# Attention with softmax differences: the sums of every second unit taken early by ScalarE, and both softmaxes joined ahead of one value product

## The chip, the cores and the metric

The kernel runs on one core of a Trainium2 chip, in fp32 throughout (some operands are rounded to fp32r and carried as a high and a low part). The metric is the device time of one execution in microseconds, the median of several runs. The engines are called as in the profile: PE (TensorE matmuls), PEld (its weight loads), DVE (VectorE), ACT (ScalarE), POOL (GpSimd) and SP (SyncE, which issues most DMAs).

## What is computed

The input x is 8 x 1024 x 512. One transformer block is applied: attention on the normalised x, added to x, then a feed-forward part on the normalised result, added again. The attention has 16 heads of width 32; each head's queries and keys are split into two halves of 16, which give two softmaxes, and their difference multiplies the values:

```python
a1 = jax.nn.softmax(jnp.einsum('bhsd,bhtd->bhst', q1, k1) * scale, axis=-1)
a2 = jax.nn.softmax(jnp.einsum('bhsd,bhtd->bhst', q2, k2) * scale, axis=-1)
lam = jnp.exp(jnp.dot(lambda_q1, lambda_k1)) - jnp.exp(jnp.dot(lambda_q2, lambda_k2)) + LAMBDA_INIT
a = a1 - lam * a2
out = jnp.einsum('bhst,bhtd->bhsd', a, v)
rms = jnp.sqrt(jnp.mean(out * out, axis=-1, keepdims=True) + EPS)
out_n = out / rms * norm_w[None, :, None, :] * (1.0 - LAMBDA_INIT)
```

The feed-forward part has ternary weights, a squared ReLU and a low-rank term. The change doesn't touch it.

## The kernel before

**Start (to 138 us).** The first batch entry is normalised, turned and projected; the feed-forward weights are made ternary and written to DRAM beside it. Under the last 16 projections the score maxima of the first two units are taken.

**The attention loop (138 to 4262 us, line 594).** A unit `u` is half the queries (512) of one head of one batch entry; there are NU = 256. Even and odd units of a head share its keys (`tk`, line 177). A unit has eight key chunks `kc` of 128 keys, and one pass of the loop, called a step here, treats two of them; so a unit has the steps kc=0, 2, 4 and 6. In each step stand, in the order in which every engine's queue gets them (the order of the code; the engines PE, ACT, DVE and POOL are not reordered, line 592):

1. `evict` (line 305) of the unit that ended in the step before: ACT copies `acc` to `avs`, scaled by 1 or -lambda.
2. `max_scores` (line 197) for the unit two ahead (AHEAD = 16 chunks): PE makes scores `mx` of 128 queries x 512 keys for both softmaxes (line 207), and DVE takes their negative maxima `nm` (line 218). The three PSUM banks of `ps_mx` go round. The second product of the first pair is put between those of `exp_scores`.
3. `exp_scores` (line 253), twice: PE adds minus the maximum (`nms`, a product with `one2`) and the transposed scores of 128 keys x 512 queries into a bank `one` (line 267; four banks, which all other work shares), and ACT writes the exponentials into `e` (line 273). No sum is taken there.
4. `add_up` (line 279): POOL adds `e` over the chunks into `es` (lines 283 and 285), three operations of 128x2048 per unit, in the steps kc=2, 4 and 6.
5. The second `max_scores` of the step.
6. In the steps kc=0 (and some kc=4): pieces of the next batch entry's preparation. Long ones are `project` (line 151, product in line 157) and `value_tile` (142, product in 145); short ones normalise and turn a tile. Further `max_turn` (230), which turns the maxima, splits them and sends them through DRAM to `nms`; `heads_out` (318) of the unit three before; and `sums` (310) of the unit two before.
7. `values` (line 296): PE multiplies the exponentials of the step before with the values. Four products of 32 output rows stand side by side in `acc` (`quarters`, line 287): two query halves for each of two softmaxes, 256 columns each.

`sums` multiplies `es` with ones, likewise in quarters. `heads_out` turns the products and the sums (four transposes), and DVE divides each softmax's part by its sum and adds the two (lines 334 to 347). Every fourth unit is followed by the RMS norm of four units: squares on ACT (358), sums on DVE, `rms_apply` on POOL (lines 368, 369 and 371, in the step kc=2 of an even unit), and `output_rows` (375) in the step kc=4 of an odd unit.

**The feed-forward part (from 4262 us).** PE runs products in lines 744 to 763, with ReLU on ACT (line 752), the square on POOL (753) and a split in two parts on DVE.

Other lines that are used below: 88 (an exponential of 128x2 on ACT), 870 (absolute values of the weights on ACT, with an accumulated sum), 877 (a fused operation of two tensors on DVE), 961 (a copy of 128x128 on ACT).

Of the kernel before, what the change touches and what calls it, by code (L numbers as in the profile page):

```python
# [24 lines left out]
def block_phases(  # L25
# [45 lines left out]
    one2 = wpool.tile([P, P], F32R, name="one2")  # L71
    nms = [wpool.tile([P, HS], F32R, name=f"nms{i}") for i in range(3)]
    for t in (one2, *nms):
        nc.gpsimd.memset(t.bitcast(F32), 0.0)
# [4 lines left out]
    def constants(stage):  # L79
        lam_in = stage.tile([P, 4, HD], F32, name="lam_in")  # L80
        for i, src in enumerate((lq1, lq2, lk1, lk2)):
            nc.sync.dma_start(lam_in[:, i, :], src.partition_broadcast(P))
        lam_pr = stage.tile([P, 2, HD], F32, name="lam_pr")
        nc.vector.tensor_mul(lam_pr, lam_in[:, 0:2, :], lam_in[:, 2:4, :])
        lam_s = stage.tile([P, 2], F32, name="lam_s")
        nc.vector.tensor_reduce(lam_s, lam_pr, AX.X, ALU.add)
        lam_e = stage.tile([P, 2], F32, name="lam_e")
        nc.scalar.activation(lam_e, lam_s, AF.Exp)

        nc.vector.tensor_sub(one_nlam, lam_e[:, 1:2], lam_e[:, 0:1])  # L90
        nc.vector.tensor_scalar_add(one_nlam, one_nlam, -LAMBDA_INIT)
        nc.vector.memset(one_nlam[0:64, :], 1.0)

        nw_in = stage.tile([P, NHP], F32, name="nw_in")
        for i in range(4):
            nc.sync.dma_start(
                nw_in[HD * i : HD * i + HD, :],
                norm_w.rearrange("(a h) d -> h d a", h=2)[i // 2],
            )
        nc.vector.tensor_scalar_mul(nw, nw_in, 1.0 - LAMBDA_INIT)  # L100
# [93 lines left out]

    nm_of, nm2_of = {}, {}

    def max_scores(u, i, apart=False):

        c, kh = divmod(i, 2)
        if i == 0:  # L200
            nm_of[u] = p_s.tile([P, 2, 2, 4], F32, tag="nm", name="nm", bufs=2)
        mx = [ps_mx.tile([P, 512], F32, tag="mx", name="mx") for _ in range(2)]
# [12 lines left out]

        def post():
            for sm in range(2):
                nc.vector.tensor_reduce(  # L218
                    nm_of[u][:, kh, sm, c : c + 1], mx[sm], AX.X, ALU.max, negate=True
                )  # L220
            if i == 7:
                nm = nm_of.pop(u)
                nm2_of[u] = p_s.tile([P, 8], F32, tag="nm2", name="nm2", bufs=2)
                nc.vector.tensor_reduce(
                    nm2_of[u], nm.rearrange("p k s c -> p (s c) k"), AX.X, ALU.min
                )

        return (lambda: product(1), post) if apart else post

    def max_turn(u):  # L230
        tr = one_bank()
        nc.tensor.transpose(tr[0:8, 0:P], nm2_of.pop(u), ident)

# [41 lines left out]
    def light(u):  # L275

        return u >= NU - 2 * H and (u % 2 == 1 or u >= NU - 3)

    def add_up(u, kc):
        e = e_of[u, kc // 2]  # L280
        if kc == 2:
            es_of[u] = p_es.tile([P, 2, 2, HS], F32, tag="es", name="es")
            nc.gpsimd.tensor_add(es_of[u], e_of[u, 0], e)  # L283
        elif kc == 4 or kc == 6 and not light(u):
            nc.gpsimd.tensor_add(es_of[u], es_of[u], e)  # L285
# [10 lines left out]
    def values(u, kc):  # L296
        b, h = divmod(u // 2, H)
        if kc == 0:
            acc_of[u] = ps_acc.tile([P, 512], F32, tag="acc", name="acc")[:, 0 : HS // 2]
        quarters(  # L300
            acc_of[u], v_of[b][:, kc, h * HD : (h + 1) * HD], e_of[u, kc // 2][:, kc % 2],
            kc == 0, kc == NS - 1,
        )

    def evict(u):
        avs_of[u] = p_s.tile([P, 2, HS // 2], F32, tag="avs", name="avs", bufs=4)

        nc.scalar.activation(avs_of[u][:, 0, :], acc_of.pop(u), AF.Copy, scale=one_nlam)

# [8 lines left out]
    def heads_out(u):  # L318

        avs = avs_of.pop(u)  # L320
        to = one_bank()
        for i in range(2):
            for c in range(2):
# [5 lines left out]
        def post():  # L329
# [6 lines left out]
            for sm, o in enumerate((parts[:, 0, 0], o2)):  # L336
# [4 lines left out]
                )  # L341
            n = u // 4
            if u % 4 == 0:
                og_of[n] = p_o.tile([P, 4, P], F32, tag="og", name="og")
            col = (u % 4) * HD
            og = og_of[n][:, :, col : col + HD]
            nc.vector.tensor_add(  # L347
# [75 lines left out]
    def first_steps():  # L423
# [6 lines left out]
        return steps  # L430

    AHEAD = 16
    def whole(step):
        post = step()
        if post:
            post()
# [3 lines left out]
    with tc.tile_pool(name="a_stage", bufs=1) as stage, tc.manual_schedule(engines=engines):  # L440
# [6 lines left out]
        for blk in range(KC):  # L447
            for which in range(2):
                cols = slice(which * E + blk * P, which * E + blk * P + P)
                nc.sync.dma_start(wqk[:, :, cols], wsrc[:, :, cols])  # L450
        pair_of = {}

# [43 lines left out]
        for i, step in enumerate(steps):  # L496
# [13 lines left out]
            if i == heads - 3:  # L510
                load_keys(0)
                load_queries(0)
            if i >= heads:
                um, im = divmod(i - heads, NS)
                if im == 0:
                    if um > 0:
                        load_keys(um // 2 + 1)
                        posts.append(max_turn(um - 1))
                    load_queries(um + 1)
                posts.append(max_scores(um, im))  # L520
            for post in posts:
                post()
        assert not others and not turns
    p_o = ctx.enter_context(tc.tile_pool(name="a_o", bufs=2))
# [63 lines left out]
    for v in range(NU):  # L588
        adds.setdefault((v + 1, 2) if light(v) else (v + 2, 0), []).append(v)
        outs.setdefault((v + 2, 0) if light(v) else (v + 3, 0), []).append(v)  # L590
    done = None
    ctx.enter_context(tc.manual_schedule(engines=engines))
    with tc.tile_pool(name="a_e", bufs=5) as p_e, tc.tile_pool(name="a_es", bufs=2) as p_es:
        for s in range(0, NS * NU + 2, 2):
            u, kc = divmod(s, NS)
            um, im = divmod(s + AHEAD, NS)
            if done is not None:
# [4 lines left out]
            if u == NU - 1 and kc == 0:  # L602
# [4 lines left out]
                )  # L607
            if um < NU:
                if im == 0 and um + 1 < NU:
                    if um % 2 == 1:  # L610
                        load_keys(um // 2 + 1)
                    load_queries(um + 1)
                between, first = max_scores(um, im, apart=True)
            else:
                between = first = None
            if u < NU:
# [7 lines left out]
                add_up(u, kc)  # L624
            reduce = max_scores(um, im + 1) if um < NU else None
            posts = []
# [5 lines left out]
            if prepare_step and long:  # L632
                posts.append(prepare_step())
            if kc == 0 and um <= NU:
                posts.append(max_turn(um - 1))
            for v in outs.pop((u, kc), []):
# [13 lines left out]
            if reduce:  # L650
                reduce()
            if 2 <= s < NS * NU + 2:
                uv, kv = divmod(s - 2, NS)
# [7 lines left out]
        evict(done)  # L661
        whole(lambda: sums(NU - 1))
    assert not later and list(adds.values()) == list(outs.values()) == [[NU - 1]]

# [401 lines left out]
def block_kernel(  # L1066
    ctx: ExitStack, tc: tile.TileContext, x, w_qkv, wo, lq1, lq2, lk1, lk2, norm_w,
    fast_b, w_fc, w_proj, u, v, gate, out,
):
    nc = tc.nc  # L1070
    B, S, E = x.shape
    cpool = ctx.enter_context(tc.tile_pool(name="consts", bufs=1))
# [41 lines left out]
```

## Time and profile before

| | |
|---|---|
| median of three runs | 5338.41 us (5337.95 to 5341.58) |
| span of the profiled execution | 5338.5 us |
| attention loop, first exponential group to the last | 138 to 4262 us, 4124 us |
| feed-forward part | 4262 to 5338 us |
| busy in the loop: PE, DVE, ACT, POOL | 4091, 3155, 2541, 3744 us |
| mean granted clock of TensorE | 0.999 |
| HBM | 60 GB/s over the span |

How to read it: the span runs from the first to the last instruction, and of the profiled execution nothing but this span is given. Busy time of PE is that of pipelined matmuls, so a full PE row means that its queue doesn't stand still, not that the array is at its peak. In a group of instructions stand the line, engine, operation, output <- inputs, partitions x elements, and the count; then the total busy time, the mean of one in ns, and how long the engine stood idle ahead of them, with what ended it. In a stretch by time, a merged row "x4" is four neighbours in a row, from the start of the first to the end of the last.

### The profile page before, as it was taken

How to read it: one execution, taken by the hardware profiler on the slowest of the kernel's cores; microseconds unless marked ns; L12 is line 12 of the kernel's file. 1: busy time of each engine (PE TensorE's matmuls, PEld its weight loads, DVE VectorE, ACT ScalarE, POOL GpSimd, SP SyncE). 2: the span in 40 equal slices, each digit the busy share in tenths (PEclk: the TensorE clock that was granted, in tenths of full speed). 3: DMA queues.
4: the chain of work that ended last, by engine and by line, in shares of the span. 5: the costliest groups of instructions: out<-in, count | busy, mean ns of one | idle time of the engine just before them, and what ended most of it. 6: DMA issues, size and time to landing. Idle time of an engine off the chain costs nothing.

```text
span 5338.5 us, 105587 instructions
## 1 busy us (share of the span) xinstructions
PE 5280.1 (99%) x41522; PEld 3243.9 (61%) x41522; DVE 3787.7 (71%) x7599; ACT 2832.5 (53%) x5502; POOL 4121.0 (77%) x1495
## 2 busy tenths in 40 slices
PE   8999999999999999999999999999999999999999
PEld 4555555555555555555555555555555578888887
DVE  6877787777778777877777777777888645555554
ACT  4665566566656665666566656655666522222221
POOL 0898899889988998899899989998888733333333
PEclk9999999999999999999999999999999999999999
DMA  8112211211121112111211121112211101111111
GB/s 275 47 55 74 71 50 55 75 66 55 54 77 65 52 57 77 64 55 56 75 65 50 60 81 57 56 61 78 100 48 44 50 31 32 32 32 32 32 32 32
DMA packets 185246, 328.48 MB, mean 62 GB/s; under 512 B 33312, under 2 KB 55840, under 8 KB 184112
## 3 DMA queue, kind: packets, MB, share of 16 engines
q1 hardware_dynamic: 183824, 319.12, 18.3%
q8 instruction: 329, 5.39, 0.4%
q0 software_dynamic: 544, 2.10, 0.1%
q14 instruction: 165, 1.35, 0.1%
q10 hardware_dynamic: 384, 0.52, 0.0%
HBM read 209.16 MB, written 112.46 MB: 60 GB/s over the span
## 4 chain that ended last, share of the span: by engine, by line
PE 84%; POOL 11%; DVE 3%; issue 1%; ACT 1%; DMA 0%; SPq 0%; POOLq 0%; DVEq 0%; ACTq 0%
PE acc L290 15%; PE one L267 14%; PE mx L207 13%; PE y L763 9%; PE pf L744 8%; PE one L157 8%; POOL es L285 6%; PE one L290 4%; PE one L145 4%; PE one L383 3%; POOL es L283 3%; PE one L324 2%; DVE nm L218 1%; PE pf L748 1%; POOL ss L369 1%
## 5 line engine op out<-in xcount | busy, mean ns | idle before, releaser
L218 DVE TENSOR_REDUCE nm<-mx 128x1 f32<-128x512 f32 x4096 | 2550.3, 683 | 256.6 <-PE mx L207 251.5
L273 ACT ACTIVATE e<-one 128x512 f32<-128x512 f32 x4096 | 2116.5, 603 | 803.2 <-PE one L267 751.1
L285 POOL TENSOR_TENSOR es<-es,e 128x2048 f32<-128x2048 f32 x495 | 2261.3, 4568 | 63.2 <-ACT e L273 31.1
L207 PE MATMUL mx<-tk,tq 64*128 64x512 f32 x4096 | 1453.1, 444 | 6.2 <-DVE nm L218 5.6
L283 POOL TENSOR_TENSOR es<-e 128x2048 f32<-128x2048 f32 x256 | 1169.6, 4569 | 278.3 <-ACT e L273 278.2
L267 PE MATMUL one<-nms,one 64*128 64x512 f32 x4096 | 1175.8, 420 | 5.1 <-ACT e L273 2.7
L290 PE MATMUL acc<-e,v 128*32 128x256 f32 x16384 | 1092.7, 384 | 0.0
L207 PEld LDWEIGHTS mx<-tk,tq 64*128 64x128 f32 x4096 | 750.9, 184 | 549.0 <-DVE nm L218 312.3
L267 PE MATMUL one<-tq,tk 64*128 64x512 f32 x4096 | 1063.6, 392 | 0.0
L753 POOL TENSOR_TENSOR r<-r 128x512 f32<-128x512 f32 x256 | 268.4, 1050 | 639.2 <-ACT r L752 618.8
L290 PEld LDWEIGHTS acc<-e,v 128*32 128x32 f32 x16384 | 450.0, 109 | 433.7 <-issue 179.0
L267 PEld LDWEIGHTS one<-tq,tk 64*128 64x128 f32 x4096 | 580.2, 185 | 82.6
L752 ACT ACTIVATE r<-pf,s_fc 128x512 f32<-128x512 f32 x256 | 176.1, 688 | 794.6 <-PE pf L748 544.2
L267 PEld LDWEIGHTS one<-nms,one 64*128 64x128 f32 x4096 | 515.2, 184 | 80.5 <-DVE og L347 15.5
L763 PE MATMUL y<-wpr,r 128*128 128x512 f32 x2048 | 523.3, 397 | 3.7 <-DVE r L757 1.7
L756 DVE CAST r<-r 128x512 fp32r<-128x512 f32 x256 | 180.4, 705 | 425.9 <-POOL r L753 425.9
L157 PE MATMUL one<-hT,wqk 128*128 128x512 f32 x1024 | 475.4, 607 | 1.5 <-ACT hT L138 1.5
L763 PEld LDWEIGHTS y<-wpr,r 128*128 128x128 f32 x2048 | 375.0, 188 | 98.6 <-DVE o L773 20.1
L744 PE MATMUL pf<-hTh,wfc 128*128 128x512 f32 x1024 | 398.8, 389 | 0.0
L744 PE MATMUL pf<-hTl,wfc 128*128 128x512 f32 x1024 | 398.6, 389 | 0.0
L165 DVE SCALAR_TENSOR_TENSOR pc<-one,pc 128x512 fp32r<-128x512 f32 x128 | 88.5, 692 | 350.9 <-ACT pc L164 350.9
L157 PEld LDWEIGHTS one<-hT,wqk 128*128 128x128 f32 x1024 | 185.0, 190 | 217.3 <-issue 187.9
(137 smaller groups left out, 4284.1 us busy)
## 6 DMA issues: line engine op xcount, KB each, us to landing
qk<-pc SPq DMA_DIRECT2D x128, 512.0 KB
tq<-qk SPq DMA_DIRECT2D x512, 128.0 KB
tk<-qk SPq DMA_DIRECT2D x256, 256.0 KB
xs<-in_L_attn_x SPq DMA_DIRECT2D x64, 256.0 KB
xr<-in_L_attn_x SPq DMA_DIRECT2D x256, 64.0 KB
x_dram<-y SPq DMA_DIRECT2D x64, 256.0 KB
out<-o SPq DMA_DIRECT2D x248, 64.0 KB
nms<-md SPq DMA_DIRECT2D x512, 4.0 KB
```

Source lines behind the costliest of these rows:

```text
L145: nc.tensor.matmul(pv, hT_of[b][:, kc, c * P : (c + 1) * P], wv[:, kc, :], start=(kc == 0), stop=(kc == KC - 1),)
L157: nc.tensor.matmul(ps, wqk[:, kc, c0 : c0 + P], hT_of[b][:, kc, tok], start=(kc == 0), stop=(kc == KC - 1),)
L207: nc.tensor.matmul(mx[sm], tq[rows, c * P : (c + 1) * P], tk[rows, kh * 512 : kh * 512 + 512], start=True, stop=True,)
L218: nc.vector.tensor_reduce(nm_of[u][:, kh, sm, c : c + 1], mx[sm], AX.X, ALU.max, negate=True)
L267: nc.tensor.matmul(st[sm], w[rows, cols], m[rows, :], start=(w is one2), stop=(w is not one2))
L273: nc.scalar.activation(e[:, kc % 2, sm, :], st[sm], AF.Exp)
L283: nc.gpsimd.tensor_add(es_of[u], e_of[u, 0], e)
L285: nc.gpsimd.tensor_add(es_of[u], es_of[u], e)
L290: nc.tensor.matmul(out[32 * g : 32 * g + 32, :], w, e[:, g // 2, (g % 2) * (HS // 2) : (g % 2 + 1) * (HS // 2)], start=start, stop=stop,)
L744: nc.tensor.matmul(pf, w[:, kc, :], hT, start=(kc == 0 and i == 0), stop=False)
L753: nc.gpsimd.tensor_mul(r, r, r)
L763: nc.tensor.matmul(ys[i], r2[:, i * P : (i + 1) * P], prep.wpr[j // (NJ // 2)][:, j % (NJ // 2), :], start=(j == 0 and k == 0), stop=(j == ...
```

## The change

Every odd unit (`normal(u)`) is treated in another way; even units stay as they were.

- **Sums taken early.** After DVE has taken the negative maximum of a block of `mx`, ACT takes the exponential of the same block in place, with that maximum as bias, and its accumulator gives the block's sum (`ss1`).
- **Sums joined to the maxima.** `join_sums` scales the two sums of a row (512 keys each) to the common maximum, adds them, takes the logarithm and subtracts it from the negative maximum. What goes through `max_turn` into `nms` is then minus the log-sum, and the exponentials of `exp_scores` are the finished softmax. `sums`, `add_up`'s adds and the division fall away.
- **The softmaxes joined.** `join_softmaxes` forms e1 - lambda e2 (`nlam` is -lambda): for the chunks of kc=0 and 6 POOL does it in two operations, queued by `add_up`; for kc=2 and 4 DVE does it in one, late in the same step. `values` then has one product: four of 32 rows and 128 columns instead of 256. `evict` is a plain copy of 128x128, and `heads_out` one transpose and one copy, two units later.
- **The order of the maxima.** Each step of the loop now has one block pair of an even unit (three units ahead) and one of an odd unit (two to three ahead), instead of two of one unit. Keys and queries are loaded four units ahead of the step, one unit earlier than before. 21 block pairs are done before the loop instead of 16.
- **Light units.** Instead of the last units of the last batch entry that skipped POOL's third add, only unit NU - 2 does.
- **One table.** ACT's function table is loaded at the start by an explicit instruction, with a set that has the exponential and the logarithm.

```diff
+    nlam = p_wo.tile([P, 1], F32, name="nlam")
...
+        nc.vector.tensor_copy(nlam, one_nlam)
...
+    def normal(u):
+        return u % 2 == 1
...
         def post():
+            nm = nm_of[u]
             for sm in range(2):
                 nc.vector.tensor_reduce(
-                    nm_of[u][:, kh, sm, c : c + 1], mx[sm], AX.X, ALU.max, negate=True
+                    nm[:, kh, sm, c : c + 1], mx[sm], AX.X, ALU.max, negate=True
                 )
+            if normal(u):
+                for sm in range(2):
+                    nc.scalar.activation(
+                        mx[sm], mx[sm], AF.Exp, bias=nm[:, kh, sm, c : c + 1],
+                        accum_out=ss1_of[u][:, kh, sm, c : c + 1],
+                    )
...
+    def join_sums(u, part):
+        nm = nm_of[u].rearrange("p k s c -> p k (s c)")
+        ss = ss1_of[u].rearrange("p k s c -> p k (s c)")
+        nm2 = nm2_of[u]
+        if part == 0:
+            dm = dm_of[u] = p_s.tile([P, 2, 8], F32, tag="dm", name="dm", bufs=2)
+            nc.vector.tensor_sub(
+                dm, nm2.rearrange("p (o x) -> p o x", o=1).to_broadcast([P, 2, 8]), nm
+            )
+            nc.scalar.activation(dm, dm, AF.Exp)
+        elif part == 1:
+            nc.vector.tensor_mul(ss, ss, dm_of.pop(u))
+            nc.vector.tensor_add(ss[:, 0], ss[:, 0], ss[:, 1])
+            nc.scalar.activation(ss[:, 1], ss[:, 0], AF.Ln)
+        else:
+            nc.vector.tensor_sub(nm2, nm2, ss1_of.pop(u).rearrange("p k s c -> p k (s c)")[:, 1])
...
     def light(u):
-        return u >= NU - 2 * H and (u % 2 == 1 or u >= NU - 3)
+        return u == NU - 2
+
+    def join_softmaxes(e, eng):
+        e1, e2 = e[:, :, 0], e[:, :, 1]
+        if eng is nc.vector:
+            eng.scalar_tensor_tensor(e1, e2, nlam, e1, ALU.mult, ALU.add)
+        else:
+            eng.tensor_scalar(e2, e2, nlam, None, ALU.mult)
+            eng.tensor_add(e1, e1, e2)
 
     def add_up(u, kc):
         e = e_of[u, kc // 2]
+        if normal(u):
+            if kc in (0, 6):
+                join_softmaxes(e, nc.gpsimd)
+            return
...
     def values(u, kc):
...
+        if normal(u):
+            for g in range(4):
+                nc.tensor.matmul(
+                    acc_of[u][32 * g : 32 * g + 32, 0:P],
+                    v_of[b][:, kc, h * HD : (h + 1) * HD],
+                    e_of[u, kc // 2][:, kc % 2, 0, g * P : (g + 1) * P],
+                    start=(kc == 0), stop=(kc == NS - 1),
+                )
+            return
...
     def evict(u):
+        acc = acc_of.pop(u)
+        if normal(u):
+            avs_of[u] = p_s.tile([P, P], F32, tag="avn", name="avn", bufs=2)
+            nc.scalar.copy(avs_of[u], acc[:, 0:P])
+            return
...
     def heads_out(u):
...
+        if normal(u):
+            nc.tensor.transpose(to[:, 0:P], avs, ident)
+            return lambda: nc.vector.tensor_copy(
+                og, to[:, 0:P].rearrange("p (g d) -> p g d", d=HD)
+            )
...
+    maxima = sorted(
+        (8 * (u // 2) * 2 + 2 * i - (17 if u % 2 else 24), u, i)
+        for u in range(NU) for i in range(NS)
+    )
+    early = [(u, i) for k, u, i in maxima if k < 0]
+    maxima = {k: (u, i) for k, u, i in maxima if k >= 0}
...
+            if kc == 0 and u + 4 < NU:
+                if u % 2 == 0:
+                    load_keys(u // 2 + 2)
+                load_queries(u + 4)
+            between = first = reduce = None
+            if s in maxima:
+                between, first = max_scores(*maxima[s], apart=True)
...
+            if kc == 0 and u % 2 == 0 and u + 1 < NU:
+                join_sums(u + 1, 2)
+            if s + 1 in maxima:
+                reduce = max_scores(*maxima[s + 1])
...
             if reduce:
                 reduce()
+                if kc == 4 and u % 2 == 1:
+                    join_sums(u + 2, 0)
+            if kc == 6 and u % 2 == 1 and u + 2 < NU:
+                join_sums(u + 2, 1)
+            if u < NU and normal(u) and kc in (2, 4):
+                join_softmaxes(e_of[u, kc // 2], nc.vector)
...
+    nc.scalar.add_instruction(
+        mybir.InstLoadActFuncSet(
+            name=nc.get_next_instruction_name(), engine=ET.Activation, act_func_set_id=6
+        )
+    )
```

## The prediction, made before the changed kernel was run

> **What bounds the kernel now.** I read the shares by engine first, then the busy times of the two stages, then the costliest groups, then single steps of the loop in order of time. A step is one pass of the loop in line 594; four make a unit, two units a pair (even, odd).
>
> Page, shares and groups (busy us, mean ns of one, idle time before):
>
> ```profile
> PE 5280.1 (99%) x41522; PEld 3243.9 (61%) x41522; DVE 3787.7 (71%) x7599; ACT 2832.5 (53%) x5502; POOL 4121.0 (77%) x1495
> ...
> L218 DVE TENSOR_REDUCE nm<-mx 128x1 f32<-128x512 f32 x4096 | 2550.3, 683 | 256.6 <-PE mx L207 251.5
> L273 ACT ACTIVATE e<-one 128x512 f32<-128x512 f32 x4096 | 2116.5, 603 | 803.2 <-PE one L267 751.1
> L285 POOL TENSOR_TENSOR es<-es,e 128x2048 f32<-128x2048 f32 x495 | 2261.3, 4568 | 63.2 <-ACT e L273 31.1
> ...
> L752 ACT ACTIVATE r<-pf,s_fc 128x512 f32<-128x512 f32 x256 | 176.1, 688 | 794.6 <-PE pf L748 544.2
> ```
>
> Busy time by stretch (PE, PEld, DVE, ACT, POOL, granted clock): the attention loop, then three stretches of the start:
>
> ```profile
> 138.00:4262.00 4124.00, 4091.21 (x36344) 2318.04 (x36346) 3154.53 (x6470) 2541.33 (x4962) 3743.88 (x1120) 1.00 0.19 62
> ```
> ```profile
> 65.00:70.00 5.00, 2.76 (x16) 1.75 (x14) 1.46 (x3) 1.84 (x2) 0.00 (x0) 0.98 0.94 294
> 70.00:75.00 5.00, 4.31 (x10) 2.65 (x11) 4.38 (x9) 2.85 (x8) 0.00 (x0) 0.50 0.77 218
> 75.00:80.00 5.00, 5.00 (x17) 2.54 (x15) 1.49 (x3) 0.92 (x2) 0.00 (x0) 0.84 0.79 268
> ```
>
> The loop takes 4124 us for 128 pairs: **32.2 us a pair**. PE is full, ACT 62%, DVE 76%, POOL 91%. ACT's idle time ends on PE. The second fence matters later: after PE stood about 2.9 us (67.8 to 70.7 us), the granted clock was 0.50.
>
> PE in order of time, plain steps and a step kc=0 with a projection:
>
> ```profile
> 2039.07 1.07 PE L290 MATMUL acc<-e,v 128*32 128x256 f32 x16
> ...
> 2041.79 1.07 PE L290 MATMUL acc<-e,v 128*32 128x256 f32 x16
> ...
> 2047.21 3.70 PE L157 MATMUL one<-hT,wqk 128*128 128x512 f32 x8
> 2050.75 0.27 PE L232 MATMUL one<-ident,nm 128*8 128x128 f32 x1
> 2050.86 0.60 PE L324 MATMUL one<-ident,avs 128*128 128x128 f32 x4
> 2051.39 1.07 PE L290 MATMUL one<-es,ones 128*32 128x256 f32 x16
> 2052.28 1.05 PE L290 MATMUL acc<-e,v 128*32 128x256 f32 x16
> 2053.26 0.49 PE L207 MATMUL mx<-tk,tq 64*128 64x512 f32 x1
> ```
>
> A plain step is 2.72 us (2039.07 to 2041.79). The long one begins with mx at 2045.50 and ends at 2053.26: 7.76 us. In a plain step ACT shows its four exponentials as 2.07 us and DVE its four reduces as 2.48 us, so both have little to spare. POOL in one unit:
>
> ```profile
> 2001.34 4.59 POOL L283 TENSOR_TENSOR es<-e 128x2048 f32<-128x2048 f32 x1 [2.01 <-ACT e L273]
> 2006.01 0.20 POOL L368 TENSOR_SCALAR ss<-ss 128x16 f32<-128x16 f32 x1
> 2006.30 2.91 POOL L369 TENSOR_TENSOR ss<-ss,neg_half 128x16 f32<-128x16 f32 x1
> 2009.29 1.05 POOL L371 TENSOR_TENSOR og<-og,ss 128x512 f32<-128x512 f32 x1
> 2010.29 9.21 POOL L285 TENSOR_TENSOR es<-es,e 128x2048 f32<-128x2048 f32 x2
> ```
>
> POOL runs far behind the exponentials it adds. That is harmless now: the sums are wanted only two units later.
>
> **The change, part by part (per pair).**
>
> *PE loses work.* A step's value product is four rounds of 0.216 us (16 matmuls, 1.00 us to the next step). At 128 columns a round costs what a 128-column transpose costs (L324: 0.11 us), so 0.57 us: 0.43 off four steps. The odd unit's sums go (0.89) and three of its four transposes (0.33). Together 2.95 us, 378 us in all, if PE still set the pace.
>
> *ACT gains 16 exponentials.* Price: four in a row took 2.07 us, the last 0.60, so 0.49 each. L752, with a pointer operand, takes 0.085 more than L273; the new bias is a pointer. For the accumulator, L870 at 42.42 us is followed by its read at 42.96 and the next instruction at 43.05: 0.09 more. So 0.67; bounds 0.49 (all hidden) and 0.89 (688 plus 199 ns, nothing overlapped). A plain step on ACT is now 4 x 0.49 + 2 x 0.67 = **3.30 us**, against PE's 2.72 (even) or 2.29 (odd). ACT sets the plain steps. It cannot make this up in long steps: the products ahead of the projection need four `one` banks and three `mx` banks, so when PE starts 3.5 us of projection, ACT has under 3 us left to do. The exponentials of `dm` and the logarithm cost some 0.2 each (L88, 128x2: 0.20). The odd eviction is a 128x128 copy (L961: 0.28), and L316's copy goes once (0.37). One table load stands in each program, so switching costs nothing.
>
> *DVE* keeps its reduces, drops one unit's five small head operations for one, and gains two joins of 128x1024 (L877, same shape: 1.28 us) plus four tiny operations (0.15 to 0.3 each). In two odd steps it has 2.48 + 1.28 = 3.76 us against ACT's 3.30. The next reduces have about 0.6 us of slack before ACT asks for them, so some 0.5 us a pair could be late. I leave it out, since POOL is later still. The moved loads run a unit earlier, as do their SP issues; nothing new waits on them. The 21 score steps before the loop (16 before) and the shorter tail cancel to within a few us.
>
> *POOL drops three odd adds and gains two joins*: one tensor-scalar and one add over 128x1024. The add is half of 4.57: 2.28. No large one-input operation is in the trace. Bounds are L368's 0.21 and the add's 2.28; I take L753's 1.05, which reads as many elements (2 x 512). Join: 3.33, bounds 2.3 and 4.6.
>
> The Trainium skill, "GPSIMD Engine Reference", section 3.1, says that one-input work runs at 1.03 cycles an element and that elementwise work belongs on VectorE. By its 1.2 GHz the first operation is an estimated 0.9 us, which takes some 20 us off the sum. No run so far shows it.
>
> *The new wait.* The odd unit's values for kc=0 and 1 now need POOL's join. They stand on PE at the end of step kc=2, before everything of step kc=4. The join stands on POOL behind three even adds. Follow one pair without the RMS work (half of them):
> - even kc=2: eviction 0.28, four exponentials 1.96: 2.24
> - POOL: 3 x 4.57 + 3.33 = 17.0 (behind plain steps of 3.30 the adds never wait)
> - PE: values 0.57, then 0.85 from the first mx to ACT's first exponential (2040.08 to 2040.92): 1.4
> - ACT, odd kc=4 and 6: 2 x 3.30 + 0.4 + 0.65 (squares, L358): 7.65
> - even kc=0: with projection 7.76 - 0.53 - 0.43 = 6.8; without, ACT's 4.6; 168 long products (112 L157, 56 L145), 28 of them in kc=4 steps, make 55% long: 5.8
>
> Sum 34.1. Where a projection stands in an even kc=4 step (28 of 64) ACT's chain is longer by about 1.1: mean 34.6. In the other half, L368, L369 and L371 stand between POOL's adds (4.17), output rows add 1.9 to kc=4, and the squares fall away: 39.5. Mean 37.05, **+4.85 a pair, +621 us**.
>
> *The clock.* In this wait PE stands 5 to 9 us in pairs with RMS work and in those whose odd kc=0 is short: 64 + 29 pairs. The row above shows 0.50 after 2.9 us. A window of a few us at half clock costs 1.7 to 3.4 us of PE work, of which ACT's pace hides about 1 us a step: I take 1.0 each, +93.
>
> The Trainium skill, "TensorE: Matmul & The Clock Gate", Part 1, gives half clock after an idle window of about 3.4 us and as long to recover. This trace was already at 0.50 after 2.9 us of idleness; by the page alone the short stalls would be free.
>
> Sum: span 5338.5 + 621 + 93 = **6050 us**. The span is the profiled execution's own time as far as shown; the median is 5338.41, 0.1 less. The same method gives 31.7 for the pair before instead of 32.2, an error of 60 us.
>
> **Rivals.**
> - *ACT sets the pace, the joins are in time* (a cheap join, or POOL ahead). Then: even kc=0 5.8, odd kc=0 5.9 (long: 7.76 - 0.89 + 0.11; short 4.6), six plain steps 19.8, evictions, `dm`, logarithm and squares 1.5, long kc=4 steps 1.5: 34.5 a pair, 2.3 more than now, **5630 us**. For it: POOL's work per pair falls from 29.2 (3743.88 / 128) to some 22 us. Against it: 13.7 us of adds cannot fit between even kc=2 and odd kc=2.
> - *Faster: PE still sets the pace.* One place, the plain step on ACT: it decides at 2.72 us, a new exponential of 0.38 or less. Then all 378 us come: **4960 us**. For it: ACT is 62% busy. Against it: the plain exponential, with no accumulator, is 0.49. (Without POOL's wait, break-even lies near 0.48: 2.3 us over twelve exponentials.)
> - *Slower than forecast*: the join takes its upper bound of 4.6 us (+160) and the half clock costs 2.3 instead of 1.0 us in 93 pairs (+120): **6330 us**.
>
> **How the numbers follow.** Forecast 0.57, joins in time 0.25, faster 0.12, slower still 0.06. The join's bounds move the sum by -130 and +160 us, the exponential's by -90 and +115. The range goes from 5500 (most of the second case) to 6300; outside stay 0.15 below and 0.05 above. Faster by over 0.2% has 0.12, within 0.2% 0.01, slower 0.87; 0.2% is about what this measurement can tell from no change.
>
> **What would show it.** In the changed profile: the new ACT group near 0.67 us a piece; plain even steps of 3.3 us; the value products of odd units waiting for POOL's add with 2 to 9 us each; PEclk below 1.00 in the loop; PE's share well under 99%. The forecast is wrong if PE's value products never wait for POOL, and its sign is wrong if plain steps stay at 2.7 us.

## The result, and the profile after

The changed kernel takes **6577.86 us** (median of four runs, 6574.87 to 6586.61), the kernel before on the same chip 5339.63 (5337.95 to 5341.58): a ratio of 1.2319 [1.2301, 1.2336]. The profiled execution has a span of 6584.8 us, 1246 more than before. From the first exponential of `exp_scores` on ACT to the last, the attention loop runs from 153.2 to 5486.3 us (140.0 to 4261.4 before): 41.7 us a pair against 32.2, which is 1212 of the 1246. The start is 13 us longer, the feed-forward part 21.

From the page of the changed kernel: shares by engine, PE's busy tenths and the granted clock in 40 slices, the chain that ended last, and groups (busy us, mean ns of one, idle time before and what ended it).

```profile
PE 5431.7 (82%) x38834; PEld 3195.5 (49%) x38834; DVE 4335.2 (66%) x7856; ACT 4116.9 (63%) x9726; POOL 3832.7 (58%) x1639
...
PE   8778877887788778877887788778877778999999
...
PEclk9889988998899889988998899889988889999999
...
PE 45%; POOL 32%; ACT 15%; DVE 3%; issue 3%; DMA 0%; SPq 0%; ACTq 0%; POOLq 0%; DVEq 0%
...
L304 ACT ACTIVATE e<-one 128x512 f32<-128x512 f32 x4096 | 2158.1, 635 | 1179.2 <-PE one L298 1174.6
...
L315 POOL TENSOR_SCALAR e<-e,nlam 128x1024 f32<-128x1024 f32 x256 | 790.7, 3089 | 1202.2 <-ACT e L304 1202.2
L231 ACT ACTIVATE mx<-mx,nm 128x512 f32<-128x512 f32 x2048 | 1406.6, 713 | 45.1 <-DVE nm L226 30.2
...
L345 PE MATMUL acc<-e,v 128*32 128x128 f32 x8192 | 383.5, 313 | 896.7 <-POOL e L316 893.4
...
L316 POOL TENSOR_TENSOR e<-e 128x1024 f32<-128x1024 f32 x256 | 601.0, 2348 | 21.4
```

No engine is full: PE's share fell from 99% to 82%, and every other one is below that. What fills the span is a chain that goes from engine to engine: PE holds 45% of it, POOL 32%, ACT 15%. L345, the value product of the odd unit, is the place: ahead of it PE stood idle for 896.7 us, and POOL's L316 ended that in 893.4. ACT has more work than before (63% of a longer span), but its idle time still ends on PE, 1174.6 us of it. The clock row shows 8 in the slices in which PE has 7.

One such place, PE first and then POOL, in order of time (start us, us, then in brackets the idle time before and what ended it):

```profile
3019.14 0.40 PE L214 MATMUL mx<-tk,tq 64*128 64x512 f32 x2
3024.91 1.08 PE L345 MATMUL acc<-e,v 128*32 128x128 f32 x16 [5.38 <-POOL e L316]
...
3028.74 0.64 PE L345 MATMUL acc<-e,v 128*32 128x128 f32 x16
```
```profile
3005.76 4.57 POOL L326 TENSOR_TENSOR es<-e 128x2048 f32<-128x2048 f32 x1 [5.09 <-ACT e L304]
3010.40 9.21 POOL L328 TENSOR_TENSOR es<-es,e 128x2048 f32<-128x2048 f32 x2
3019.57 2.86 POOL L315 TENSOR_SCALAR e<-e,nlam 128x1024 f32<-128x1024 f32 x1
3022.51 2.34 POOL L316 TENSOR_TENSOR e<-e 128x1024 f32<-128x1024 f32 x1
```

POOL starts the even unit's adds at 3005.76 and works with gaps of no more than 0.1 us until the join ends at 3024.85. PE goes on 0.06 us later. The adds are wanted only two units later, but they stand ahead of the join in POOL's queue. The first 16 products after the wait take 1.08 us, the next ones 0.64. The stretches (PE, PEld, DVE, ACT, POOL, granted clock) show why:

```profile
3020.00:3025.00 5.00, 0.09 (x4) 0.10 (x8) 2.14 (x3) 2.09 (x6) 4.83 (x3) 0.68 0.01 2
3025.00:3030.00 5.00, 5.00 (x49) 3.17 (x49) 2.54 (x4) 2.54 (x5) 0.97 (x3) 0.64 0.00 0
```

Over the whole loop, PE stands before the odd unit's first value products 3.5 us on average in the 65 pairs without the RMS work (0 to 6.8), and 9.8 us in the 63 pairs with it. TensorE was at half clock for 1073 us of the span (18 us before), 1051 of them in the loop; 539 of these fall into times in which PE stood idle.

### The profile page after: what moved, and what is told of

It reads as the page before. It is cut to its first block, busy times and chain, and to the rows that moved or that the text cites. A ratio compares the mean times of both kernels' runs of the same rounds, so it can differ in the third digit from the quotient of the medians.

```text
span 6584.8 us, 105215 instructions
## 1 busy us (share of the span) xinstructions
PE 5431.7 (82%) x38834; PEld 3195.5 (49%) x38834; DVE 4335.2 (66%) x7856; ACT 4116.9 (63%) x9726; POOL 3832.7 (58%) x1639
## 4 chain that ended last, share of the span: by engine, by line
PE 45%; POOL 32%; ACT 15%; DVE 3%; issue 3%; DMA 0%; SPq 0%; ACTq 0%; POOLq 0%; DVEq 0%
POOL es L328 12%; ACT e L304 9%; POOL e L315 7%; PE y L851 7%; PE pf L832 7%; PE mx L214 6%; PE one L159 6%; PE one L298 5%; ACT mx L231 5%; POOL e L316 5%; POOL es L326 4%; PE one L446 4%; PE acc L345 3%; PE one L147 3%; POOL ss L432 3%
## 5 line engine op out<-in xcount | busy, mean ns | idle before, releaser
L304 ACT ACTIVATE e<-one 128x512 f32<-128x512 f32 x4096 | 2158.1, 635 | 1179.2 <-PE one L298 1174.6
L298 PE MATMUL one<-nms,one 64*128 64x512 f32 x4096 | 1449.2, 465 | 53.1 <-ACT e L304 29.5
L315 POOL TENSOR_SCALAR e<-e,nlam 128x1024 f32<-128x1024 f32 x256 | 790.7, 3089 | 1202.2 <-ACT e L304 1202.2
L231 ACT ACTIVATE mx<-mx,nm 128x512 f32<-128x512 f32 x2048 | 1406.6, 713 | 45.1 <-DVE nm L226 30.2
L328 POOL TENSOR_TENSOR es<-es,e 128x2048 f32<-128x2048 f32 x255 | 1159.2, 4546 | 18.0 <-ACT e L304 4.5
L345 PE MATMUL acc<-e,v 128*32 128x128 f32 x8192 | 383.5, 313 | 896.7 <-POOL e L316 893.4
L326 POOL TENSOR_TENSOR es<-e 128x2048 f32<-128x2048 f32 x128 | 584.6, 4567 | 607.8 <-ACT e L304 607.8
L345 PEld LDWEIGHTS acc<-e,v 128*32 128x32 f32 x8192 | 230.5, 121 | 1088.7 <-POOL e L316 957.6
L316 POOL TENSOR_TENSOR e<-e 128x1024 f32<-128x1024 f32 x256 | 601.0, 2348 | 21.4
L333 PE MATMUL acc<-e,v 128*32 128x256 f32 x8192 | 548.5, 385 | 0.0
L231 ACT ACTIVATION_READ_ACCUMULATOR mx<-mx,nm 128x1 f32 x2048 | 525.0, 256 | 0.0
L313 DVE SCALAR_TENSOR_TENSOR e<-e,nlam 128x1024 f32<-128x1024 f32 x256 | 485.5, 1896 | 13.9 <-ACT e L304 12.7
```

Source lines behind the costliest of these rows:

```text
L231: nc.scalar.activation(mx[sm], mx[sm], AF.Exp, bias=nm[:, kh, sm, c : c + 1], accum_out=ss1_of[u][:, kh, sm, c : c + 1],)
L298: nc.tensor.matmul(st[sm], w[rows, cols], m[rows, :], start=(w is one2), stop=(w is not one2))
L304: nc.scalar.activation(e[:, kc % 2, sm, :], st[sm], AF.Exp)
L315: eng.tensor_scalar(e2, e2, nlam, None, ALU.mult)
L316: eng.tensor_add(e1, e1, e2)
L345: nc.tensor.matmul(acc_of[u][32 * g : 32 * g + 32, 0:P], v_of[b][:, kc, h * HD : (h + 1) * HD], e_of[u, kc // 2][:, kc % 2, 0, g * P : (g ...
```

## The experiments

Each kernel is the changed one with the edit shown, compared with the kernel before on the same chip. Line numbers are those of each run's own kernel. "kc=2: 6.88, 13.31" stands for the mean time of the odd unit's step kc=2 in pairs without and with the RMS work; those two values and 3.46, 7.53 for kc=4 are the changed kernel's. (In the changed kernel the RMS work on POOL is queued in the step kc=2 of an even unit and `output_rows` in kc=4 of an odd one. The description of the kernel before gives the same places, but in that kernel each of the two stands one unit later.) The theories, as the expectations number them:

1. PE waits for a join that stands behind the even unit's adds in POOL's queue (the forecast).
2. ACT's 16 added exponentials set the pace.
3. The half clock after the waits is itself a large part.
4. DVE's operations with two inputs in SBUF and POOL's operations exclude each other, so the joins cost more than their own time.

**Is it the queue?** The join of kc=0 is put ahead of the even unit's third add.

```diff
         if normal(u):
             if kc in (0, 6):
                 join_softmaxes(e, nc.gpsimd)
+            if kc == 0 and not light(u - 1):
+                nc.gpsimd.tensor_add(es_of[u - 1], es_of[u - 1], e_of[u - 1, 3])
             return
...
-        elif kc == 4 or kc == 6 and not light(u):
+        elif kc == 4:
```

> POOL's join of the odd unit's first chunks is queued ahead of the even unit's third add instead of behind it; nothing is left out. Theory 1 (PE waits for POOL's queue): the join ends 4.57 us earlier, the wait before the odd unit's first value products falls from a mean of 4.0 and 9.6 us (units without and with RMS work on POOL) to about 0 and 5, the half clock becomes rarer, and the time falls by 500 to 700 us, to some 6000. Theory 2 (ACT's added exponentials set the pace everywhere): the time stays within 100 us of 6578.

Measured: 6194.7 us, 1.1599 [1.1582, 1.1616]: 383 us less, with the same work. The step kc=2 fell by 2.8 and 5.6 us (to 4.04, 7.68), and PE's waits for POOL's join from 893.4 to 374.8 us (in total, times, longest):

```profile
PE acc L347 <- POOL e L316: 374.8, 128, 5.9
```

Theory 2 foresaw no change, so it doesn't set this time. The 500 to 700 us that were expected of theory 1 were missed: less came back than the 4.57 us of the moved add, since without the RMS work kc=4 rose from 3.46 to 6.00: the add now runs beside DVE's join of the step kc=2 (L313, 3.8 us in the mean of these pairs, up to 5643 ns).

**Is it ACT?** The added exponentials are left out (the sums are set to 1), the joins kept.

```diff
+                nc.vector.memset(ss1_of[u], 1.0)
...
-            if normal(u):
-                for sm in range(2):
-                    nc.scalar.activation(
-                        mx[sm], mx[sm], AF.Exp, bias=nm[:, kh, sm, c : c + 1],
-                        accum_out=ss1_of[u][:, kh, sm, c : c + 1],
-                    )
```

> Leaves out ACT's 16 added exponentials (the sums are set to 1) and keeps all joins. Theory 1 (POOL's chain of three adds and the join sets the pair, whatever ACT does): even steps become shorter, the wait longer by as much, and only the steps after the wait gain: 6578 falls by no more than 300 us, to 6300 or above. Theory 2 (ACT's pace): it falls by as much as without joins, some 600 us, to about 6000.

Measured: 6599.3 us, 1.2353 [1.2334, 1.2371]. ACT lost 1307 us of work (4116.9 to 2810.4 us busy), and nothing was gained. The waits view (us in total, times, longest) tells where it went:

```profile
PEld acc L340 <- POOL e L311: 1172.2, 158, 13.4
...
PE acc L340 <- POOL e L311: 1111.8, 158, 13.0
```

PE's wait rose from 893.4 to 1111.8 us, the longest from 11.4 to 13.0. PE came earlier and POOL no sooner. The time at half clock rose too, from 1073 to 1306 us; by the experiment with idle products below, where 804 us less of it were worth some 107 us in the steps behind the wait, that is an estimated 30 us, far from the 600 that theory 2 asks for. Theory 1 is shown, theory 2 refuted for this kernel.

**What do the joins cost in all?** All four joins of an odd unit are left out, so its second softmax is missing from the output.

```diff
-            if kc in (0, 6):
-                join_softmaxes(e, nc.gpsimd)
...
-            if u < NU and normal(u) and kc in (2, 4):
-                join_softmaxes(e_of[u, kc // 2], nc.vector)
```

> Leaves out all four joins, on POOL and DVE: the odd unit's value products take the first softmax alone. Theory 1: with no wait for POOL only ACT's added exponentials are left, 34.5 us a pair as in the forecast's second case, 5630; from the step times of the changed kernel (even plain steps only 0.1 us longer than before) rather 5500. Theory 2: the time stays over 6300. If neither ACT nor POOL mattered, 4960.

Measured: 5574.84 us, 1.0436 [1.042, 1.0451], 33.8 us a pair. The joins and what they set off cost 1003 us. What is left is the rival "joins in time", for which the prediction had 34.5 a pair and 5630 us.

**And then ACT?** The joins and the added exponentials are both left out (the two edits above).

> Leaves out all four joins and also ACT's 16 added exponentials (the sums are set to 1). What is left is the changed order with less PE work. Theory 2 (with the joins away, ACT's added exponentials are what keeps the kernel above the one before): PE sets the pace again and the price of the forecast's faster case is reached, about 4960 (4930 to 5050); against 5575 with the exponentials they cost some 600 us. If the new order of the maxima itself costs time: over 5150.

Measured: 5138.29 us, 0.962 [0.9605, 0.9634]. That lies between the two expectations (4930 to 5050, or over 5150). With the wait gone the exponentials cost 437 us (some 600 were expected); with the wait there they cost nothing. The saving on PE alone is 201 us of the 378 that its removed products and sums would give. In the chain that ended last, PE holds 73%, and by line DVE's reduces come first:

```profile
PE 73%; DVE 21%; issue 3%; ACT 1%; POOL 0%; DMA 0%; DVEq 0%; SPq 0%; ACTq 0%; POOLq 0%
DVE nm L227 15%; PE mx L215 12%; PE one L293 11%; PE y L842 9%; PE pf L823 9%; PE one L159 9%; PE acc L326 7%; PE one L147 4%; PE one L439 3%; PE acc L338 3%; PE one L326 2%; PE pf L827 1%; ACT e L299 1%; DVE bs L123 1%; DVE one L398 1%
```

So, taken away in this order, the change comes to 1238 us as 1003 (joins and their wait) + 437 (exponentials) - 202 (PE's saving). In another order the parts differ: the exponentials alone come to nothing.

**Is it the half clock?** Idle products keep PE busy through the wait (12 or 33 per odd unit, into a free bank).

```diff
+            if u < NU and normal(u) and kc == 2:
+                busy = one_bank()
+                for _ in range(12 if u % 4 == 1 else 33):
+                    nc.tensor.matmul(
+                        busy, tq_of[u][:, 0:P], tk_of[u // 2][:, 0:512], start=True, stop=True
+                    )
```

> Adds idle matmuls (12 or 33 of 128x512, about 2.6 or 7.1 us at full clock) on PE just ahead of the odd unit's first value products, inside the time in which PE waits there; the result goes nowhere. Theory 3 (the half clock after the wait costs much): the granted clock rises to near 1.00 in the loop and the time falls by 150 to 350 us although PE does more. If the half clock is hidden by ACT's pace: the time stays within 60 us or rises.

Measured: 6527.93 us, 1.2219 [1.2201, 1.2238], 50 us less. The time at half clock fell from 1073 to 269 us. The steps kc=4 after the wait fell to 2.71 and 6.61 (0.83 a pair, 107 us), while kc=2 without the RMS work rose to 7.60, where the idle products outlasted a short wait. So theory 3 is worth about 100 us, and the idle products cost about half of it again. In the changed kernel half of the half clock (539 of 1051 us in the loop) falls where PE has nothing to do; that ACT's pace hides much of the rest is argued, not shown.

**Which half of POOL's join?** POOL's multiplication is left out (the second softmax is added with the factor 1).

```diff
         else:
-            eng.tensor_scalar(e2, e2, nlam, None, ALU.mult)
             eng.tensor_add(e1, e1, e2)
```

> Leaves out the multiplication by -lambda in POOL's two joins (chunks 0, 1, 6 and 7 of odd units), the operation that was put at 1.05 us and took 2.85 us. Theory 1: every wait becomes 2.85 us shorter where it is that long, 2.85 x 128 = 365 us, and with less half clock 400 to 500: some 6100 to 6180. Theory 2: no change beyond 100 us.

Measured: 6502.85 us, 1.2175 [1.2155, 1.2196]; the expectation was missed. The step kc=2 did fall, by 2.2 and 3.0 us (4.71, 10.33). But the even unit's kc=0 rose from 7.70, 7.18 to 10.24, 8.49: of some 330 us, 246 were lost again. DVE and PE of this run in order of time:

```profile
3045.57 2.22 DVE L255 TENSOR_TENSOR ss<-ss 128x8 f32<-128x8 f32 x1
3047.72 1.27 DVE L226 TENSOR_REDUCE nm<-mx 128x1 f32<-128x512 f32 x2
```
```profile
3048.45 0.49 PE L214 MATMUL mx<-tk,tq 64*128 64x512 f32 x1 [1.23 <-DVE nm L226]
...
3048.87 5.40 PE L147 MATMUL one<-wv,hT 128*128 128x512 f32 x8
```

The 128x8 add of `join_sums` takes 0.17 us when alone, and 2.22 here (over 1 us in 62 of 128 cases): POOL's add of kc=6, no longer preceded by the multiplication, runs at that moment. The reduces behind it are late, PE stands for 1.23 us, and the long product that follows runs partly at half clock (from 3049.4 to 3052.8 us): 5.40 us for what took 3.70 in the changed kernel. Shortening one link moved another into a collision.

**Two-input operations on DVE beside POOL.** DVE's two joins (kc=2 and 4) are left out, and with them this part of the second softmax; POOL's stay.

```diff
-            if u < NU and normal(u) and kc in (2, 4):
-                join_softmaxes(e_of[u, kc // 2], nc.vector)
```

> Leaves out the two joins on DVE (chunks 2 to 5 of odd units take the first softmax alone); POOL's stay. Theory 4 (operations of two SBUF inputs on DVE and POOL exclude each other): POOL's multiplication loses its 3.8 us cases, the wait in units with RMS work becomes 1 us shorter, and small steps after it gain: 6578 falls by 60 to 150 us. If there is no such exclusion: within 30 us of 6578, as DVE has time to spare in the wait.

Measured: 6495.35 us, 1.2156 [1.2138, 1.2174], 83 us less, as expected of theory 4. POOL's multiplication is the row to look at:

```profile
L315 POOL TENSOR_SCALAR e<-e,nlam 128x1024 f32<-128x1024 f32 x256 | 729.0, 2848 | 1178.1 <-ACT e L304 1178.1
```

It is 2848 ns now (2833 to 2862 in all 256), against 3089 in the changed kernel, where 63 of 256, those of the odd unit's first join in the pairs with the RMS work, took 3.82 us. The two sides of one such meeting in the changed kernel, an RMS pair, DVE and then POOL:

```profile
3058.99 4.08 DVE L313 SCALAR_TENSOR_TENSOR e<-e,nlam 128x1024 f32<-128x1024 f32 x1
```
```profile
3052.84 9.15 POOL L328 TENSOR_TENSOR es<-es,e 128x2048 f32<-128x2048 f32 x2
3061.96 3.82 POOL L315 TENSOR_SCALAR e<-e,nlam 128x1024 f32<-128x1024 f32 x1
```

DVE's join, 1.28 us when alone, is issued in the middle of POOL's add and ends 1.08 us after it; then POOL's multiplication is 1 us too long. By these times each waits for the other's whole instruction. The Trainium skill, "SBUF — State Buffer", section "SBUF: two separate sides", says that VectorE and GpSimd share a pair of ports that is locked for a whole instruction, when a VectorE operation has two SBUF inputs and the GpSimd operation reads SBUF. The 4.08 and 3.82 us here agree.

**All joins on DVE.** Theory 1 alone would let this come close to the kernel without joins, theory 4 not.

```diff
-            if kc in (0, 6):
-                join_softmaxes(e, nc.gpsimd)
...
-            if u < NU and normal(u) and kc in (2, 4):
+            if u < NU and normal(u):
```

> All four joins on DVE (one operation of 1.28 us each), none on POOL; nothing is left out. Theory 1 alone: the wait for POOL's queue is gone, DVE has 2.6 us more a pair: 5600 to 5700. Theory 4 (an operation of two SBUF inputs on DVE and one on POOL exclude each other, as the 4.1 to 5.1 us of some joins on DVE beside POOL's adds suggest): a join on DVE that meets an add on POOL lasts up to 4.6 us longer, holds the reduces behind it, and the time is over 5800.

Measured: 6178.85 us, 1.1566 [1.1549, 1.1583]. L313 in this run (shortest, median and longest in ns, first and last start):

```profile
L313 DVE SCALAR_TENSOR_TENSOR e<-e,nlam x512: 1262/1278/5115, 172.0 to 5088.1; 128x1024 f32<-128x1024 f32 x171
```

The mean is 2028 ns. The long ones are those of the odd unit's kc=0 (4.0 and 4.6 us in the mean, without and with the RMS work), beside POOL's long adds; the other three joins of a unit take 1.28. DVE's next operations come late by it, and PE waits for DVE instead (for the operations of `max_turn` 246.6 us, for the reduces 137.3). Theory 4 is shown.

**What the forms of POOL's multiplication cost.** For kc=0 the factor is an immediate (-0.5 in place of -lambda), for kc=6 it is a broadcast tensor. This kernel ran twice.

```diff
-            if kc in (0, 6):
-                join_softmaxes(e, nc.gpsimd)
+            if kc == 0:
+                nc.gpsimd.tensor_scalar(e[:, :, 1], e[:, :, 1], -0.5, None, ALU.mult)
+                nc.gpsimd.tensor_add(e[:, :, 0], e[:, :, 0], e[:, :, 1])
+            if kc == 6:
+                nc.gpsimd.tensor_mul(
+                    e[:, :, 1], e[:, :, 1],
+                    nlam.rearrange("p (a o) -> p a o", a=1).to_broadcast([P, 2, HS]),
+                )
+                nc.gpsimd.tensor_add(e[:, :, 0], e[:, :, 0], e[:, :, 1])
```

> POOL's multiplication ahead of its two joins in two other forms: for kc=0 by an immediate (-0.5, which stands for -lambda and changes the result), for kc=6 by a broadcast tensor of two inputs. It is there for the durations in the trace. If the pointer operand makes the 2.85 us, the immediate form takes 0.9 to 1.2 us and the wait before the odd unit's values falls by 1.7 us: some 6250 to 6400. If it is the tensor-scalar operation itself, both durations stay above 2.3 us and the time stays near 6578. The two-input form should take the add's 2.35.

Measured: 6731.09 us, 1.2599 [1.2573, 1.2624]. The groups (busy us, mean ns):

```profile
L322 POOL TENSOR_SCALAR e<-e 128x1024 f32<-128x1024 f32 x128 | 416.6, 3255 | 0.0
...
L325 POOL TENSOR_TENSOR e<-e,nlam 128x1024 f32<-128x1024 f32 x128 | 242.3, 1893 | 1210.2 <-ACT e L304 1210.2
```

The immediate doesn't make the one-input form cheaper (median 2.79 us, up to 3.77); the two-input form with a broadcast is, at 1.89 us. The kernel became slower all the same, by 153 us: kc=0 of the even unit rose to 9.20, 7.85, which is 139 of them. There the add of kc=6 comes earlier and again meets DVE's small operations (L258, 1212 ns in the mean against 158 in the changed kernel, and L255, 938 against 569).

**Without joins, but complete.** The odd unit's values are scaled by -lambda once per unit, and `values` makes eight products of 128 columns into the same accumulator; all joins go, and `avn` has one buffer instead of two. First the scaling stands on DVE:

```diff
...
+            if kc == 0:
+                vl_of[u] = p_s.tile([P, NS, HD], F32, tag="vl", name="vl", bufs=1)
+                nc.vector.tensor_scalar_mul(vl_of[u], vh, nlam)
+            for sm, w in enumerate((vh, vl_of[u])):
+                for g in range(4):
+                    nc.tensor.matmul(
+                        acc_of[u][32 * g : 32 * g + 32, 0:P], w[:, kc, :],
+                        e_of[u, kc // 2][:, kc % 2, sm, g * P : (g + 1) * P],
+                        start=(kc == 0 and sm == 0), stop=(kc == NS - 1 and sm == 1),
+                    )
...
```

> No join on any engine: the odd unit's values are scaled once by -lambda (DVE, 128x256), and each chunk has eight value products of 128 columns, four for each softmax, into one sum; nothing is left out. PE gets 0.43 us a step back in odd units. Theory 1 and 2 together: the wait is gone, ACT's pace hides most of PE's 1.73 us a pair: 5575 to 5650. If PE set the pace: 5575 + 221 = 5800.

Measured: 6022.76 us, 1.1273 [1.1254, 1.1292]; missed. The waits:

```profile
PEld acc L348 <- DVE vl L345: 327.4, 127, 5.1
...
PE acc L348 <- DVE vl L345: 293.2, 127, 4.9
```

L345 is an operation of 128x256 with one input in SBUF. It takes 340 ns when alone, up to 4137, 1431 in the mean: it too stood behind POOL's operations (the 62 that took over 0.5 us all end 0.15 us behind one). So theory 4, which speaks of two inputs, is too narrow. Then the same with the scaling on ACT, in the step kc=4 of the even unit:

```diff
...
+    def scale_values(u):
+        b, h = divmod(u // 2, H)
+        vl_of[u] = p_s.tile([P, NS, HD], F32, tag="vl", name="vl", bufs=1)
+        nc.scalar.activation(
+            vl_of[u], v_of[b][:, :, h * HD : (h + 1) * HD], AF.Copy, scale=nlam
+        )
...
```

> As e8_scaled_values, with the multiplication of the values by -lambda moved from DVE, ahead of the odd unit's first products, to ACT in the even unit's step kc=4; nothing is left out. Theory 1: the wait is really gone; what remains is ACT's added exponentials as without joins, and PE's 1.73 us a pair is partly hidden: 5575 to 5700, and the granted clock above 0.98. If e8's 6020 came from its eight products instead of from the late multiplication: over 5900.

Measured: 5664.21 us, 1.0603 [1.0587, 1.0618], as expected, 34.5 us a pair. PE no longer waits for POOL or DVE at `acc`; the time at half clock is 18 us. It is the best complete kernel that treats every second unit, and slower than the kernel before. ACT holds 32% of the chain that ended last (PE 60%), and the two exponential lines on ACT lead it by line (17% and 14%); that ACT's exponentials set its pace is read from this chain and from the 437 us above, and not tested in this kernel.

**Every fourth unit.** The last kernel with only the units u % 4 == 1 treated (and the light units of the kernel before), to let PE's lead cover ACT.

```diff
     def normal(u):
-        return u % 2 == 1
+        return u % 4 == 1
...
```

> As e11_scaled_by_act, with every fourth unit instead of every second; nothing is left out. PE saves the sums and three transposes of 64 units, 1.22 us each, 78 us. If ACT's added exponentials cost as much for each such unit as without joins (437 us for 128, 3.4 us each): 5340 - 78 + 218 = 5480. If ACT makes up for them in the steps without: 5260 to 5330, faster than both kernels.

Measured: 5574.29 us, 1.0432 [1.0415, 1.045]; missed on the slow side. Half the exponentials bring 90 us back, not half of the 322 by which the last kernel is slower than the one before. The steps tell where the time goes. In the units u % 4 = 0 and 1 they last as long as in the kernel before, within 0.1 us a unit; the units 2 and 3, in which ACT's added exponentials stand, are 1.0 and 2.2 us longer, some 200 us of the 232 in all. PE's weight loads wait for ACT's added exponentials there (195.3 us); their wait for DVE's maxima (283.6) is no longer than in the kernel before (312.3). The largest single step, kc=6 of unit 3 with 1.0 us, is also the one in which the difference `dm` on DVE, 175 ns when alone, takes 1112 in the mean, now that POOL adds in three of four units. How much of that step is ACT's and how much is this meeting is not settled. No complete version beat the kernel before.

## Why the prediction came out as it did

The direction and the main mechanism were right: PE waits at the odd unit's first values for a join behind POOL's adds, and the clock drops. The time was 6578 instead of 6050, outside the range. The chain of the prediction, term by term (us, pairs without / with the RMS work):

| term | predicted | measured |
|---|---|---|
| POOL's first add to the start of the join | 13.7 / 17.9 | 13.86 / 18.02 |
| multiplication of the join | 1.05 | 2.85 / 3.81 |
| add of the join | 2.28 | 2.35 |
| end of the join to ACT's next exponential | 1.4 | 2.33 |
| odd kc=4 to the next even kc=0 | 7.65 / 8.9 | 7.76 / 10.56 |
| even kc=0 to POOL's next first add | 8.0 | 8.55 / 8.75 |
| sum | 34.1 / 39.5 | 37.7 / 45.8 |

The prediction added 0.5 to the first sum for projections in kc=4, and 0.73 a pair for the clock: 37.8 us in the mean. By the loop's length the pair took 41.7.

- **The step that failed: "Bounds are L368's 0.21 and the add's 2.28; I take L753's 1.05".** The multiplication took 2.85 us, more than the upper bound, and 3.81 where DVE's join met it: 2.3 us a pair too little, some 290 of the 528 us along the chain. (Leaving the multiplication out gained only 75 us, since its absence caused the collision in the even unit's kc=0; so the 290 are a sum over the measured chain, not a difference of two runs.) The bound held that one input can't cost more than two; the experiment with the forms shows that it does (2.85 against 1.89 for the broadcast). The estimate of 0.9 us that the prediction worked out from the Trainium skill, "GPSIMD Engine Reference", section 3.1, was further off still; the measurement decides.
- **"I leave it out, since POOL is later still"** (the DVE joins) failed too. They cost 83 us. Some 62 of these are POOL's join, held up by 1 us in the pairs with the RMS work, and not DVE being late. The prediction treated DVE and POOL as independent.
- **The clock** was named with 1.0 us in 93 of 128 pairs. By the table, the terms behind the wait are 0.9 (end of the join to ACT's next exponential), 0.9 (odd kc=4 on, in the mean of both kinds of pair) and 0.6 us (even kc=0) longer than predicted, against 0.73 foreseen. The idle products recovered 0.83. So it was about the right size for the clock itself. With idle products the first of the three falls from 2.33 to 1.61 us in pairs with the RMS work, so most of its excess there is the half clock; what is left of the other two is not settled.
- **ACT's part of the chain** fits in size by luck. The prediction put four of the added exponentials, 2.7 us a pair, into the term "odd kc=4 and 6" (7.65, measured 7.76 without the RMS work). In the kernel without any of them the same term still takes 7.3 us, and 10.5 against 10.6 with the RMS work. Something else holds these steps nearly as long. The half clock and DVE's joins have a share, as idle products or the absence of these joins shorten the term by 0.2 to 0.6 us each; the whole of it is not settled.
- **ACT's 0.67 us** for a new exponential was right: in the changed kernel two of them start at 3005.54 and 3006.20. The **plain step of 3.30** comes only late in a run of steps: the even unit's plain steps took 2.7 to 3.3 us, as it seems because PE's lead is used up first. It cost nothing in the sum, because POOL is later.
- **The rivals' prices**: "joins in time" was 5630, the kernel without joins took 5575. "PE still sets the pace" was 4960, the kernel without joins and exponentials took 5138: the saving on PE is 201 us, not 378. The "slower still" rival named the right two terms, a dearer join and more half clock, and was still too low by 248 us.
- **The range** ended at 6300, since the join's upper bound was taken for a bound. With 2.85 and 3.81 in the same sum the forecast would have been 6340 (1.8 and 2.76 us more, a mean of 2.28 in 128 pairs). The join's lower bound of 2.3 is a slip as well: 0.21 and 2.28 add up to 2.5.

## What to carry to other kernels

In an in-order queue a consumer pays for everything that stands ahead of its producer: before work is moved to the engine "with room", write down what is queued there when the result is wanted, and move the urgent piece ahead first (383 us here for no change of work). Price an operation only from a row of that operation on that engine, and where there is none, leave the upper end open, as fewer inputs are no proof of less time. Count VectorE's operations with two SBUF inputs, and a scaling from SBUF to SBUF, as users of one resource with GpSimd's operations, down to the smallest ones: a 128x8 add stood for 2 us behind a GpSimd operation, and whatever waits in its queue stands with it.

## What the runs showed of the hardware

- A POOL multiplication of 128x1024 with one tensor takes 2.85 us with a pointer and 2.79 with an immediate (median); the add of two tensors takes 2.35, the product with a broadcast column 1.89.
- DVE operations on tiles in SBUF that met a running POOL operation ended only after it had ended: up to 5.6 us for a join of 1.28, 2.22 for a 128x8 add of 0.17, and 4.1 for a one-input scaling of 0.34. DVE's reduces, which read PSUM, show nothing of this (685 ns against 683 before).
- In the changed kernel's loop the granted clock fell to half in stretches of 3.4, 6.8, 10.2 or 13.7 us. Each of the 100 idle times of PE over 4 us had such a stretch, starting in it or within 3.5 us behind it, and none of the 13 of 1.5 to 2 us had one. But in the kernel without POOL's multiplication one began 0.9 us behind two short idle times of 0.38 and 1.23 us. Getting rid of 804 us of half clock with idle products gained 50 us, net of what the products cost.
